# The feed-forward's first product by seven block products in place of eight (decoder layer, one core)

## The chip, the cores and the metric

The kernel runs on one core of a Trainium2 chip. The metric is the device time of one execution in microseconds. The engines are TensorE (PE, with its weight loads PEld), VectorE (DVE), ScalarE (ACT), GpSimd (POOL) and SyncE (SP), which issues most transfers. Each works through its own list of instructions in order and waits at semaphores for the others.

## What is computed

One decoder layer on 8 batches of 256 tokens, width 1024, all in float32: self-attention with sign weights, cross-attention through a low rank, and a low-rank feed-forward, each on a normalised input and added to its stream. The change touches the feed-forward alone:

```python
x = x + _L0_ffn_ref(_layernorm(x, axis=-1), U1, V1, U2, V2, b1, b2)

P = jnp.einsum('bsh,hr->bsr', x, U1)          # 1024 -> 256
H = jnp.einsum('bsr,rf->bsf', P, V1) + b1     # 256 -> 2 x 2752
gate, up = (H[..., :INTER], H[..., INTER:])
act = jax.nn.silu(gate) * up
Z = jnp.einsum('bsi,ir->bsr', act, U2)        # 2752 -> 256
out = jnp.einsum('bsr,rh->bsh', Z, V2) + b2   # 256 -> 1024
```

The product with V1 is the "first product" here: its inner size, 256, is two blocks of 128 (r = 0, 1), and gate and up (i = 0, 1) are two blocks of its rows for each of 21 full groups f of 128 hidden units and one half group of 64.

## The kernel before

**Order.** The program is written under a manual schedule: every engine runs its instructions in the order in which the Python code emits them. Self-attention of all batches comes first, then cross-attention in steps of four heads, then the feed-forward. `step` runs one such step; lists of `Part`s (`cross_plan`) are worked off inside it, so that work of a later stage stands between.

**Feed-forward before.** Tokens go in four blocks of 512 (`fbs`, W = 512). `ffn_x` loads a block's rows of x2 from DRAM. `head_parts` makes its input: `first` normalises the rows on VectorE (`normed_half`, L157), sends them to a DRAM buffer (L1063) and reads them back in quarters (L168); `turn` transposes them in 32x32 squares on VectorE (L1088, 128x512 each); `factor` multiplies by u1 into `ps_p` (L1103) and copies the result to `pT` (even blocks) or `late` (odd blocks).

**One hidden group.** `hidden(fb, k)` takes two PSUM tiles `ps_h` (gate and up) of 512 columns, each the sum of two products, r = 0 and 1 (L1134). ScalarE takes the sigmoid of the gate (L1146), VectorE two three-operand steps on the PSUM tiles (L1147, L1149) that give `ac`. `down` multiplies `ac` by u2 into `ps_z0` and `ps_z1`, which gather over all groups (L1178); the half group is treated by `down_half` (L1158). The main loop keeps `hidden` two groups ahead of `down` (`lag = 2`).

**Tails.** After a block's last group its two `ps_z` are copied to SBUF (L1191); `tail` multiplies by v2 (L1198), adds the token row, to which GpSimd has added b2 (L1480), on VectorE (L1206), and sends it out (L1207). The tails of a block stand between the first groups of the next.

**PSUM.** Eight banks in four pools: `pss` with four buffers (the scores, later `ps_h`), `psA` with two (token products, tails), `psB` and `pso` with one each (`ps_z`).

**Where names recur.** A tile is taken from a pool under a tag; taking a tag again waits until every reader of the tile that held it is done. The tags `qw0` to `qw7` are 128x1024 buffers of 512 KB, in which the token rows stand.

Of the kernel before, what the change touches and what calls it, by code (L numbers as in the profile page):

```python
# [18 lines left out]
P = 128  # L19
# [16 lines left out]
def decoder_layer(  # L36
# [118 lines left out]
    def normed_half(x_, mv, rs, h, tag="xn"):  # L155
        xn = wk_.tile([P, 512], F32, tag=tag, name="xn", bufs=2)
        nc.vector.tensor_scalar(  # L157
            xn, x_[:, h * 512 : (h + 1) * 512], mv, rs, ALU.subtract, ALU.mult
        )
        return xn  # L160
# [862 lines left out]
    def ffn_load_u2():  # L1023
        for k in range(4):
            u2_load(k, xin.tile([P, E], F32, tag="xin", name="u2_sb"))

    def ffn_load_end():
        for k in range(4, (NF + 3) // 4):
            u2_load(k, wk_.tile([P, E], F32, tag=("oh0a", "oh0b")[k - 4], name="u2_sb"))
# [13 lines left out]
    def ffn_x(fb):  # L1043
        while idle:
            idle.pop(0)()
        fb.x = []
        for j in range(BT):
            xs = wt.tile([P, E], F32, tag=f"qw{4 * ((fb.i + 1) % 2) + j}", name="x2t")
            nc.sync.dma_start(xs, x2[fb.i * BT + j])
            fb.x.append(xs)  # L1050

    def head_parts(fb):


        def send(j):
            b = fb.i * 2 + j // TB
            need(fb.half[j // TB])
            for h in range(2):
                xn = normed_half(
                    fb.x[j], mv3[b][:, j % TB, 0:1], rs3[b][:, j % TB : j % TB + 1], h,  # L1060
                    "z" if j % 2 else "xn",
                )
                nc.sync.dma_start(n3[fb.i * BT + j][:, h * 512 : (h + 1) * 512], xn)  # L1063

        def first(m):
            for j in range(2 * m, 2 * m + 2):
                send(j)
            if fb.i == 0 and m == 1:
# [6 lines left out]
            fb.xp = getattr(fb, "xp", {})  # L1075
# [4 lines left out]
        def turn(m):  # L1080
            if m == 0:
                fb.xT = [
                    wk_.tile([P, 4, W], F32, tag="qT", name="xT0", bufs=2),
                    wk_.tile([P, 4, W], F32, tag="xl", name="xT1"),
                ]
            for j in range(2 * m, 2 * m + 2):
                for h in range(2):
                    nc.vector.transpose(  # L1088
                        fb.xT[h][:, :, j * P : (j + 1) * P].rearrange("p c (a q) -> p c a q", q=32),
                        fb.xp[m][j % 2].rearrange("p a (c e) -> p c a e", e=32)[  # L1090
                            :, 4 * h : 4 * h + 4
                        ],
                    )

        def factor(r):
            if r == 0:
                if fb.i % 2 == 0:
                    fb.pT = [wk_.tile([P, W], F32, tag="v", name="pT", bufs=2) for _ in range(RC)]
                else:
                    fb.pT = [fw.late[:, k, :] for k in range(RC)]  # L1100
            ps = psA.tile([P, W], F32, tag="psA", name="ps_p")
            for e in range(EC):
# [3 lines left out]
                    fb.xT[e // 4][:, e % 4, :],  # L1106
# [3 lines left out]
            (dve if r else act)(fb.pT[r], ps)  # L1110

        order = (0, 2, 1, 3) if fb.i == 0 else (0, 1, 2, 3)
        ln = [
            Part(0.0, lambda: first(0)),
            Part(0.0, lambda: turn(0)),
            Part(0.0, lambda: first(1)),
            Part(0.0, lambda: turn(1)),
        ]
        return [ln[k] for k in order] + [Part(7.0, lambda r=r: factor(r)) for r in range(RC)]

    order = list(range(FULL))
    order[FULL - 3 : FULL - 3] = range(FULL, NF)

    def hidden(fb, k):
        f = order[k]
        n = P if f < FULL else LAST
        halves = COPIES if f == FULL else 1
        w_ = W // halves
        hs = []
        for i in range(2):  # L1130
            ps = pss.tile([P, w_], F32, tag="pss", name="ps_h")
            for r in range(RC):
                for h in range(halves):
                    nc.tensor.matmul(  # L1134
                        ps[h * n : h * n + n],
                        v1_of(r, i, f, n),
                        fb.pT[r][:, h * w_ : (h + 1) * w_],
# [4 lines left out]
        m = n * halves  # L1142
        bg = fw.b1[:m, f : f + 1]
        bu = fw.b1[:m, NF + f : NF + f + 1]
        sg = wk_.tile([P, w_], F32, tag="p", name="sg", bufs=4)
        nc.scalar.activation(sg[:m], hs[0][:m], AF.Sigmoid, bias=bg)  # L1146
        nc.vector.scalar_tensor_tensor(sg[:m], hs[0][:m], bg, sg[:m], ALU.add, ALU.mult)  # L1147
        ac = wk_.tile([P, w_], F32, tag="pT", name="ac", bufs=4)
        nc.vector.scalar_tensor_tensor(ac[:m], hs[1][:m], bu, sg[:m], ALU.add, ALU.mult)  # L1149
        return ac, n  # L1150

    def down_half(fb, cross):

        ac, n = fb.half_ac
        w_ = W // COPIES
        for h in range(COPIES):
            r = (h + cross) % RC
            nc.tensor.matmul(  # L1158
                fb.zs[r][:, h * w_ : (h + 1) * w_],
                fw.u2[FULL // 4][h * n : h * n + n, FULL % 4, r * P : (r + 1) * P],  # L1160
                ac[h * n : h * n + n],
                start=False,
                stop=bool(cross),
            )

    def down(fb, k, ac, n):
        if k == 0:
            fb.zs = [
                pso.tile([P, W], F32, tag="pso", name="ps_z0"),
                psB.tile([P, W], F32, tag="psB", name="ps_z1"),  # L1170
            ]
        f = order[k]
        if f == FULL and COPIES == 2:
            fb.half_ac = ac, n
            down_half(fb, 0)
            return
        for r in range(RC):
            nc.tensor.matmul(  # L1178
                fb.zs[r],
                fw.u2[f // 4][:n, f % 4, r * P : (r + 1) * P],  # L1180
                ac[:n],
                start=(k == 0),
                stop=(k == NF - 1 and COPIES < 2),
            )
        if k == NF - 1:
            if COPIES == 2:

                down_half(fb, 1)
            fb.zT = fw.late[:, RC : 2 * RC, :]
            for r, copy in enumerate((dve, act)):  # L1190
                copy(fb.zT[:, r, :], fb.zs[r])  # L1191

    def tail(fb, j, pieces=((0, 512), (512, 512))):
        for c0, n in pieces:
            cols = slice(c0, c0 + n)
            ps = psA.tile([P, n], F32, tag="psA", name="ps_o")
            for r in range(RC):
                nc.tensor.matmul(  # L1198
                    ps,
                    fb.zT[:, r, j * P : (j + 1) * P],  # L1200
# [4 lines left out]
            xs = fb.x[j][:, cols]  # L1205
            nc.vector.tensor_add(xs, ps, xs)  # L1206
            nc.sync.dma_start(of[fb.i * BT + j][:, cols], xs)  # L1207
# [89 lines left out]
    o7, rest, hp0 = [], [], []  # L1297

    def cross_plan(b):
        late = list(rest)  # L1300
        if b + 1 == B:
            return [late + hp0[1:3], hp0[3:4], hp0[4:5], hp0[5:6]]
# [8 lines left out]
        else:  # L1311
            plan = [late + c, k + ln[1:], q + (o[b + 1] if b < 3 else [])]
        rest[:] = u[2:]
        if b + 2 == B:
            hp0[:] = head_parts(fbs[0])
        return plan + [t + u[:2] + (lnx(b + 2)[:1] if b + 2 < B else hp0[:1])]
# [37 lines left out]
    def cross_loads(b, c):  # L1354
        if c == 1 and b + 2 < B:
            cross_c(xts[b + 2])
        if c == 0:
# [5 lines left out]
            if b == 5:  # L1363
                ffn_load_u2()
        if b == B - 2 and c == 2:
            ffn_x(fbs[0])
            ffn_load_v2()
        if b == B - 1 and c == 3:
            ffn_load_b(1)

    with tc.manual_schedule(
# [77 lines left out]
        pairs = [(fb, f) for fb in fbs for f in range(NF)]  # L1449
        acs = {}  # L1450

        def hidden_next(n):
            acs[n] = hidden(*pairs[n])

# [3 lines left out]
        fw.late = None  # L1458
        hidden_next(0)
        prev.weighted(pTs)  # L1460
        hidden_next(1)
        prev.early()
        prev.late()
        ffn_load_end()
        fw.late = wt.tile([P, 2 * RC, W], F32, tag="vw", name="late")
        settle()
        settle()
        lag = 2
        for n in range(2, len(pairs) + lag):
            fb, f = pairs[n] if n < len(pairs) else (None, n)  # L1470
            if fb is not None:
                hidden_next(n)
                if fb.i == 0 and f == 3:
                    x_leave(xts[B - 1])
                elif idle:
                    idle.pop(0)()
                if 10 <= f < 10 + BT:

                    xs = fb.x[f - 10]
                    nc.gpsimd.tensor_add(xs, xs, fw.b2)  # L1480
                if fb.i + 1 < NB:
                    if f == 6:
                        ffn_x(fbs[fb.i + 1])
                    if f == 8:
                        hp = head_parts(fbs[fb.i + 1])
                        queue.extend(hp)
                        queue[0].ahead()
                    for _ in range({9: 1, 11: 2, 13: 1, 14: 1, 15: 1}.get(f, 0)):
                        run_part()
            m = n - lag  # L1490
# [40 lines left out]
```

## Time and profile before

| | us |
|---|---|
| median of three runs (1511.9 to 1512.79) | 1512.69 |
| the profiled execution's own time | 1512.69 |
| its span, from the first to the last instruction | 1510.6 |
| feed-forward in the span (first `ps_h` product to the end) | 957.5 to 1510.6 |
| TensorE busy in the span | 1472.3 |
| VectorE, ScalarE, GpSimd busy | 980.9, 786.3, 398.2 |
| mean granted TensorE clock | 0.997 |

In a row of the groups or the timeline, `out<-in` are the program's tile names; after the shapes come how many, the busy time, the mean duration in ns, and the idle time of the engine before them with what ended it. A row of the timeline begins with its start and its duration in us and merges neighbours ("x2"). A product of 128x128 weights with 512 float32 columns stands in the trace as two matmul records.

### The profile page before, as it was taken

To read this page: it belongs to the slowest core of one execution; us is meant where nothing else is said; L and a number is where in the kernel's file an instruction comes from. 1 tells how busy PE (TensorE), PEld (TensorE's weight loads), DVE (VectorE), ACT (ScalarE), POOL (GpSimd) and SP (SyncE) were. 2 spreads that over 40 slices of the span, in tenths; PEclk is the share of its full clock that TensorE was granted. 3 is DMA by queue.
4 is the path that set the end of the run, shared out by engine and by line. 5 is a ranking of instruction groups with operands and counts; after the bars stand their busy time and mean duration, and the time that the engine had idled before them with its cause. 6 is when DMAs were issued, how large, how long until landed. Compare 5 with 4: busy or idle time off the path is not lost.

```text
span 1510.6 us, 25435 instructions
## 1 busy us (share of the span) xinstructions
PE 1472.3 (97%) x9118; PEld 981.2 (65%) x9118; DVE 980.9 (65%) x1911; ACT 786.3 (52%) x2429; POOL 398.2 (26%) x472
## 2 busy tenths in 40 slices
PE   6899999999999999899999999999999999999999
PEld 6777888888888886677777776444444444444444
DVE  6888898999999888867787776354335233523332
ACT  4778898989898987746566666310111110111110
POOL 2544454535453545123231211141002000200000
PEclk9999999999999999999999999999999999999999
DMA  8520020101010134334486755132014002300001
GB/s 214 122 57 30 15 71 29 57 30 57 30 62 24 57 106 154 101 98 116 142 259 207 198 169 164 63 97 57 0 64 152 7 15 97 112 0 28 28 0 56
DMA packets 102958, 126.33 MB, mean 84 GB/s; under 512 B 44539, under 2 KB 75441, under 8 KB 102705
## 3 DMA queue, kind: packets, MB, share of 16 engines
q1 hardware_dynamic: 98224, 107.94, 24.8%
q0 software_dynamic: 4608, 16.78, 2.8%
q8 instruction: 72, 1.18, 0.3%
q14 instruction: 54, 0.43, 0.1%
HBM read 82.21 MB, written 41.94 MB: 82 GB/s over the span
## 4 chain that ended last, share of the span: by engine, by line
PE 55%; ACT 2%; DVE 2%; DMA 1%; issue 0%; SPq 0%; ACTq 0%; DVEq 0%
PE ps_h L1134 20%; PE ps_z L1178 10%; PE ps_pt L579 4%; PE ps_o L1198 4%; PE ps_p L1103 4%; PE s L676 3%; PE po L699 3%; PE ps_o L716 2%; PE ps_q L925 2%; ACT p L762 2%; PE ps_qk L941 2%; PE ps_k L855 1%; PE ps_o L547 1%; DMA n<-xn 0%; PE ps_z L1158 0%
## 5 line engine op out<-in xcount | busy, mean ns | idle before, releaser
L762 ACT ACTIVATE p<-s,nm 128x256 f32<-128x256 f32 x768 | 359.0, 519 | 4.4 <-DVE nm L743 4.4
L1146 ACT ACTIVATE sg<-ps_h,b_col 128x512 f32<-128x512 f32 (+1 forms) x88 | 59.6, 678 | 427.6 <-PE ps_h L1134 427.5
L583 ACT COPY pT<-ps_pt 128x512 f32<-128x512 f32 x384 | 197.4, 599 | 147.0 <-PE ps_pt L579 147.0
L743 DVE TENSOR_REDUCE nm<-s 128x2 f32<-128x512 f32 x384 | 237.2, 676 | 4.6 <-PE s L676 3.4
L1147 DVE SCALAR_TENSOR_TENSOR sg<-ps_h,b_col,sg 128x512 f32<-128x512 f32 (+1 forms) x88 | 64.8, 736 | 241.9 <-ACT sg L1146 241.9
L579 PE MATMUL ps_pt<-ident,p 128*128 128x128 f32 x1536 | 197.4, 280 | 7.3 <-ACT pT L583 2.8
L579 PEld LDWEIGHTS ps_pt<-ident,p 128*128 128x128 f32 x1536 | 165.9, 142 | 47.8 <-issue 24.3
L762 ACT ACTIVATION_READ_ACCUMULATOR p<-s,nm 128x1 f32 x768 | 192.7, 251 | 0.0
L1178 PE MATMUL ps_z<-ac,u_sb 128*128 128x512 f32 x336 | 158.0, 593 | 0.0
L454 PE MATMUL ps_q<-xh,qT_w 128*128 128x256 f32 x496 | 121.7, 287 | 0.0
L454 PE MATMUL ps_q<-xl,qT_w 128*128 128x256 f32 x496 | 118.8, 281 | 0.0
L1178 PEld LDWEIGHTS ps_z<-ac,u_sb 128*128 128x128 f32 x336 | 63.5, 190 | 80.0 <-issue 80.0
L1480 POOL TENSOR_TENSOR x2t<-x2t,b_sb 128x1024 f32<-128x1024 f32 x16 | 38.8, 2436 | 272.3 <-DVE xn L157 272.3
L547 PE MATMUL ps_o<-oT_w,oh 128*128 128x512 f32 x256 | 105.5, 412 | 0.0
L731 POOL TENSOR_TENSOR x1t<-x1t,y 128x256 f32<-128x256 f32 x64 | 46.2, 742 | 221.2 <-DVE y L724 221.2
L407 POOL TENSOR_SCALAR tmp<-y 128x512 f32<-128x512 f32 x78 | 58.5, 751 | 166.3 <-DVE y L556 91.2
L547 PE MATMUL ps_o<-oT_w,ol 128*128 128x512 f32 x256 | 101.0, 395 | 0.0
L454 PEld LDWEIGHTS ps_q<-xh,qT_w 128*128 128x128 f32 x496 | 93.3, 188 | 1.7
L454 PEld LDWEIGHTS ps_q<-xl,qT_w 128*128 128x128 f32 x496 | 93.4, 188 | 0.0
L623 DVE TENSOR_SCALAR p<-p,sm 128x256 f32<-128x256 f32 x256 | 86.8, 396 | 8.4 <-PE ps_q L454 0.5
L1134 PE MATMUL ps_h<-pT,w_ffn 128*128 128x512 f32 (+1 forms) x184 | 88.7, 577 | 0.0
L1134 PE MATMUL ps_h<-late,w_ffn 128*128 128x512 f32 (+1 forms) x184 | 88.7, 577 | 0.0
(156 smaller groups left out, 2648.5 us busy)
## 6 DMA issues: line engine op xcount, KB each, us to landing
xs<-in_x_dram SPq DMA_DIRECT2D x32, 512.0 KB
n<-xn SPq DMA_DIRECT2D x64, 256.0 KB
xp<-n SPq DMA_DIRECT2D x128, 128.0 KB
x<-xs POOLq DMA_DIRECT2D x16, 512.0 KB, 3.1
x1t<-x SPq DMA_DIRECT2D x16, 512.0 KB
c<-in_ctx_dram SPq DMA_DIRECT2D x64, 128.0 KB
x<-x1t POOLq DMA_DIRECT2D x16, 512.0 KB, 5.3
x2t<-x SPq DMA_DIRECT2D x16, 512.0 KB
```

Source lines behind the costliest of these rows:

```text
L454: nc.tensor.matmul(ps[:, i, :], w(i, e), x_[:, e, :], start=(e == 0 and x_ is st.xh), stop=(e == EC - 1 and x_ is st.xl),)
L547: nc.tensor.matmul(ps, o_[c // 4][:, c % 4, t * P : (t + 1) * P], oT_w[:, c, h * 512 : (h + 1) * 512], start=(c == 0 and o_ is st.oh), sto ...
L579: nc.tensor.transpose(ps[:, k, t * P : (t + 1) * P], p[:, t, k * P : (k + 1) * P], ident)
L583: nc.scalar.copy(pT, ps)
L623: nc.vector.tensor_scalar_mul(p, p, self.sm[:, t, j : j + 1])
L743: nc.vector.tensor_reduce(nm[:, j, :], s[j], AX.X, ALU.max, negate=True)
L762: nc.scalar.activation(cur.p[j][:, t, :], s[j][:, t, :], AF.Exp, bias=nm[:, j, t : t + 1], accum_out=cur.sm[:, t, j : j + 1],)
L1103: nc.tensor.matmul(ps, fw.u1[:, e, r * P : (r + 1) * P], fb.xT[e // 4][:, e % 4, :], start=(e == 0), stop=(e == EC - 1),)
L1134: nc.tensor.matmul(ps[h * n : h * n + n], v1_of(r, i, f, n), fb.pT[r][:, h * w_ : (h + 1) * w_], start=(r == 0), stop=(r == RC - 1),)
L1147: nc.vector.scalar_tensor_tensor(sg[:m], hs[0][:m], bg, sg[:m], ALU.add, ALU.mult)
L1178: nc.tensor.matmul(fb.zs[r], fw.u2[f // 4][:n, f % 4, r * P : (r + 1) * P], ac[:n], start=(k == 0), stop=(k == NF - 1 and COPIES < 2),)
L1198: nc.tensor.matmul(ps, fb.zT[:, r, j * P : (j + 1) * P], fw.v2[:, r, cols], start=(r == 0), stop=(r == RC - 1),)
```

## The change

The feed-forward goes over two blocks of 1024 tokens (`dbs`), each two halves of 512. With A the 2x2 blocks of V1 (gate and up by r) and B the 2x2 blocks of P (r by half), the four results are formed from seven products (Winograd's form of Strassen's scheme) by `unit`. Sums of weight blocks are formed on GpSimd one unit ahead (`weight_sums`), sums of token blocks once for each 1024 tokens on VectorE (`sums`). Three of the products gather in one PSUM tile `c21`, which ScalarE reads out between them. In the listing `act` is a ScalarE copy, `stt` a VectorE three-operand step, `mul` a GpSimd multiplication:

```python
def weight_sums(db, f):
    ...
    g.tensor_add(s_[:, 0, :], a[1][0], a[1][1])
    g.tensor_sub(s_[:, 1, :], s_[:, 0, :], a[0][0])
    g.tensor_sub(s_[:, 2, :], a[0][0], a[1][0])
    g.tensor_sub(s_[:, 3, :], a[0][1], s_[:, 1, :])

def sums(db):
    ...
    sub(db.t1, b12, b11)
    sub(db.t2, b22, db.t1)
    sub(db.t3, b22, b12)
    sub(db.t4, b21, db.t2)

def unit(db, k, following):
    ...
    extra = max(0, len(zq) - 4)
    product(c21, v1_of(0, 0, f, P), b11, True, False)      # c21a
    act(a1, c21)
    product(c11, v1_of(1, 0, f, P), b21, True, True)       # c11
    trailing()
    stt(g1, c11, bg, a1, ALU.add, ALU.add)
    fill(1 + (extra > 0))
    product(c21, s_[:, 1, :], db.t2, False, False)         # c21b
    nc.scalar.activation(sg1, g1, AF.Sigmoid)
    act(q, c21)
    product(c12, s_[:, 0, :], db.t1, True, False)          # c12a
    fill(1 + (extra > 1))
    product(c21, s_[:, 2, :], db.t3, False, False)         # c21c
    act(q7, c21)
    mul(g1, g1, sg1)
    stt(ac2, c12, bu, q7, ALU.add, ALU.add)
    if following is not None:
        weight_sums(*following)
    fill()
    product(c21, v1_of(1, 1, f, P), db.t4, False, True)    # c21d
    stt(g1, c21, bu, g1, ALU.add, ALU.mult)
    fill()
    product(c12, s_[:, 3, :], b22, False, True)            # c12b
    stt(g2, c12, bg, q, ALU.add, ALU.add)

    def rest():
        nc.scalar.activation(sg2, g2, AF.Sigmoid)
        mul(g2, g2, sg2)
        mul(ac2, ac2, g2)

    trail.append(rest)
    for t, ac in ((0, g1), (1, ac2)):
        for r in range(RC):
            zq.append(lambda t=t, r=r, ac=ac: down(db, k, r, t, ac))
```

(The names behind the products are added here for reference.) `fill` issues the next waiting product with u2 from `zq`; `trailing` emits the `rest` of the unit before. The half group (`half_unit`) stays a direct product, now over 2 x 512 tokens. The four `ps_z` of 1024 tokens take `psA`, `psB` and `pso`; token products and tails move to `pss`. Transposes become 128x128 pieces; the normalisation of the first two blocks of 512 moves to GpSimd and to the last two cross-attention steps' lists, that of the others stays on VectorE, with the tag `xn` (two buffers) alone. The rows of x2 are loaded a second time for the tails:

```diff
+    def tail_x(db, j, tag):
+        xs = wt.tile([P, E], F32, tag=tag, name="x2t")
+        nc.sync.dma_start(xs, x2[db.i * 2 * BT + j])
+        nc.gpsimd.tensor_add(xs, xs, fw.b2)
+        db.x = getattr(db, "x", {})
+        db.x[j] = xs
```

The main loop after the change:

```diff
-        lag = 2
-        for n in range(2, len(pairs) + lag):
...
+            return {
+                2: lambda: x_leave(xts[B - 1]),
+                4: lambda: ffn_x(fbs[2], 0),
+                5: lambda: f2[0].main(),
+                6: lambda: ffn_x(fbs[2], 1),
+                7: lambda: (turns(t2_, 0), f2[1].main()),
+                9: lambda: turns(t2_, 1),
+                10: lambda: ffn_x(fbs[3], 0),
+                11: lambda: (p2[0].main(), f3[0].main()),
+                12: lambda: (p2[1].main(), ffn_x(fbs[3], 1)),
+                14: lambda: (turns(t3_, 0), f3[1].main()),
+                16: lambda: turns(t3_, 1),
+            }.get(k, lambda: None)
+
+        for k in range(FULL):
+            if k == FULL - 3:
+                half_unit(d0)
+            unit(d0, k, (d0, units[k + 1]) if k + 1 < FULL else (d1, units[0]))
+            if idle:
+                idle.pop(0)()
+            between(k)()
+        trailing()
+        for j in range(3):
+            tail_x(d0, j, f"qw{j}")
+        p3[0].main()
+        p3[1].main()
+        for k in range(FULL):
+            if k == FULL - 3:
+                half_unit(d1)
+            unit(d1, k, (d1, units[k + 1]) if k + 1 < FULL else None)
+            if 1 <= k < 1 + 2 * BT:
+                tail(d0, k - 1)
+                if k + 2 < 2 * BT:
+                    tail_x(d0, k + 2, f"qw{(k + 2) % 3}")
+            if 12 <= k < 16:
+                tail_x(d1, k - 12, ("qw0", "qw1", "qw2", "qw4")[k - 12])
+        for j in range(4, 8):
+            tail_x(d1, j, ("qw3", "qw5", "qw6", "qw7")[j - 4])
+        trailing()
+        fill(len(zq))
+        for j in range(2 * BT - 1):
+            tail(d1, j)
+        tail(d1, 2 * BT - 1, ((0, 512), (512, 256), (768, 128), (896, 128)))
```

Here `f2`, `t2_`, `p2` are the normalisation, transposes and token products of the third block of 512, `f3`, `t3_`, `p3` those of the fourth. Of the second block of 1024, the first half's b11 and b21 stand in `qw3`, b12 and b22 in `qw5`, the sums t1 and t3 in `qw6`, t2 and t4 in `qw7`.

## The prediction

> **What bounds the kernel now.** I read the page's head and the stretches first, then the chain that ended last, then the timeline of one hidden unit, then the groups on GpSimd, and last the DMA issues.
>
> ```profile
> span 1510.6 us, 25435 instructions
> PE 1472.3 (97%) x9118; PEld 981.2 (65%) x9118; DVE 980.9 (65%) x1911; ACT 786.3 (52%) x2429; POOL 398.2 (26%) x472
> ```
> ```profile
> 1050.00:1100.00 50.00, 50.00 (x133) 21.93 (x132) 14.36 (x20) 6.56 (x10) 0.00 (x0) 1.00 0.00 0
> 1450.00:1511.00 61.00, 56.85 (x155) 25.44 (x153) 18.02 (x27) 5.87 (x9) 0.00 (x0) 0.99 0.09 35
> ```
>
> The columns of a stretch are its length, then the busy time of PE, PEld, DVE, ACT and POOL. From 950 us on this is the feed-forward: TensorE never rests, VectorE works 30% of the time, ScalarE 13%, GpSimd nearly nothing. A matmul taken out there is time saved, as long as nothing else becomes late.
>
> ```profile
> 1210.43 1.02 PE L1134 MATMUL ps_h<-late,w_ffn 128*128 128x512 f32 x2
> 1210.63 0.69 ACT L1146 ACTIVATE sg<-ps_h,b_col 128x512 f32<-128x512 f32 x1 [4.01 <-PE ps_h L1134]
> 1211.29 1.02 PE L1134 MATMUL ps_h<-late,v1b 128*128 128x512 f32 x2
> 1211.35 0.75 DVE L1147 SCALAR_TENSOR_TENSOR sg<-ps_h,b_col,sg 128x512 f32<-128x512 f32 x1 [3.62 <-ACT sg L1146]
> 1212.14 1.88 PE L1178 MATMUL ps_z<-ac,u_sb 128*128 128x512 f32 x4
> ```
>
> A product of 128x128 by 512 columns is two records, and products start 0.86 us apart (1210.43, 1211.29). A reader starts 0.20 us after the issue of the product ends (the product before 1210.43 gates the 1210.63). Release of TensorE by VectorE costs 0.06: copy of ps_z ends 1493.24, next matmul 1493.30.
>
> **What goes.** 21 full units x 2 blocks of 1024 tokens x 1 product = 42 x 0.86 = 36.0 us. The half unit took 1205.01 to 1206.89, 1.88 x 4 = 7.5, and its second product 0.63 x 8 = 5.0; now they are 8 and 4 pairs of 0.86, 10.3 together: 2.2 less. The 0.8 us in which the last product waits for the copy of ps_z goes too, as other work now stands between. Removed: **39.0 us**.
>
> **One unit, step by step.** TensorE's order in it, starts from 0: c21a 0, c11 0.86, z 1.72, c21b 2.57, c12a 3.43, z 4.29, c21c 5.15, z 6.01, c21d 6.86, z 7.72, c12b 8.58, end 9.44. The z are the last unit's products with u2. Durations: ScalarE copy from PSUM 0.59 (ps_z, L1191), sigmoid 0.69, VectorE's three-operand step 0.75, GpSimd as below.
>
> ```profile
> L408 POOL TENSOR_TENSOR z<-z,tmp 128x512 f32<-128x512 f32 x32 | 42.5, 1329 | 2.7
> L1480 POOL TENSOR_TENSOR x2t<-x2t,b_sb 128x1024 f32<-128x1024 f32 x16 | 38.8, 2436 | 272.3 <-DVE xn L157 272.3
> ```
>
> So a multiplication of 128x512 on GpSimd is 1.32, an addition of 128x1024 2.36 (its median), a weight sum of 128x128 some 0.45 (0.742 at 256 columns, 1.329 at 512).
> - ScalarE: copy a1 1.06 to 1.65; the trailing sigmoid of the unit before to 2.34 (its input is ready at 1.1 + 0.2); sg1 after g1 (VectorE 1.92 to 2.67), 2.7 to 3.39; copy q 3.63 to 4.22; copy q7 6.21 to 6.80.
> - c21b may start when a1 is read: 0.9 us to spare. c21c needs q: 0.9 to spare. c21d needs q7: 6.86 against 6.86, nothing to spare.
> - GpSimd: the two trailing multiplications 2.4 to 5.0, g1 to 6.4, four weight sums to 8.2. The third z needs the trailing result: 5.0 against 6.01.
>
> A unit thus fits in 9.44. Only the tight q7 costs: bounds 0 and 0.3 x 42 = 12 us, I take 0.05 x 42 = **2**.
>
> **VectorE between the units of the first block of 1024.** Normalisation and transposes for the second are put behind units 5, 7, 9, 11, 14 and 16, ahead of the next unit's g1, sg1 and q, which queue in this order. A burst of X starts at 0.95 of the next unit (behind g2), so q ends at 0.95 + X + 0.75 + 0.03 + 0.69 + 0.59 = 3.0 + X, and c21c, due at 5.15, stalls X - 2.1.
>
> ```profile
> 1149.07 3.94 DVE L157 TENSOR_SCALAR xn<-x2t,mv,rs 128x512 f32<-128x512 f32 x4
> 1150.20 2.53 POOL L1480 TENSOR_TENSOR x2t<-x2t,b_sb 128x1024 f32<-128x1024 f32 x1 [121.67 <-DVE xn L157]
> ```
>
> Four normalised halves took 3.94 while GpSimd was at work (median of one 0.54, so 2.2 alone). Now GpSimd works in every unit and the halves have two buffers, not four; I take 3.9, bounds 2.2 and 5.5 (twice the wait seen). The transposes become 16 of 128x128 for 4 of 128x512 (0.62 each in a row): between a quarter of it, 2.5, and a 128x128 copy each, 16 x 0.28 = 4.5; I take 16 x 0.22 = 3.5. Statistics add 0.7 to the first.
> - behind 5: 4.6, stalls 2.5; behind 7 and 14: 7.4, stalls 5.3 each; behind 9 and 16: 3.5, stalls 1.4 each; behind 11 a token product of 6.9 us on TensorE covers it. Together **16**, bounds 5 and 28. This cover was there before: a unit's results were wanted two units later.
>
> [...]
>
> **The first unit** has no z to fill with, and its g1 stands behind four VectorE sums and y (0.8 + 2.6 + 0.7 = 4.1 after the last token product), the table load of 1.28 (once in the trace) and sg1: q ends at 7.3, c21c was due at 4.6 (1.15 of ps_o and four products); then c21d waits 0.9. **3.6**, bounds 2 and 6.
>
> **The tails of the first block of 1024.** Behind units 1 to 5 of the second block stand a tail of token tile k-1 (four products, 3.43), then a load of x2 into the buffer that this tail just emptied, and GpSimd's addition of b2 to it. On GpSimd this addition stands ahead of the trailing multiplications, for which the third z of the next unit waits.
>
> ```profile
> 1129.52 0.69 DVE L1206 TENSOR_TENSOR x2t<-ps_o,x2t 128x512 f32<-128x512 f32 x1 [0.95 <-PE ps_o L1198]
> ```
> ```profile
> 1130.66 2.13 SPq L1049 DMA_DIRECT2D x2t<-x  x4
> ```
> ```profile
> 4.26 1.29 DVE L140 BATCH_NORM_STATS2 st<-xs 128x6 f32<-128x512 f32 x2 [4.26 <-DMA xs<-in_x_dram]
> ```
>
> The last addition ends at 1130.21; the last of four loads into those buffers is issued by about 1132.4, so an output of 256 KB lands within 2.2. A load of 512 KB: issued at 0.73 at the kernel's start, first read at 4.26: 3.5; bounds 2.2 (the output) and 5.3 (GpSimd's own 512 KB writes, the page's median). From the unit's end: tail 3.43, its last addition 3.63 to 4.32, output landed 6.6, load landed 10.15, b2 added 12.55, two multiplications 15.2. The third z is due at 3.43 + 6.01 = 9.44: a stall of 5.8 us, five times = **29**; with the bounds 22 and 38.
>
> [...]
>
> **The end.** Four such additions stand ahead of the last unit's two trailing multiplications. The second of their loads goes into the buffer of b12 and b22, which c12b frees at 9.44: landed 13.1, three additions to 20.2, multiplications to 22.8. The third z was due at 9.44 + 1.72 = 11.16. **11.7**, bounds 10 and 15; nothing is behind it but the tails, which wait for it.
>
> **Elsewhere.** The token products of the second half block move into the last cross step; they use the score buffers and wait for the exponentials (0.8 each, twice), and the second block's first q is late by 0.4: **2**, bounds 0 and 5. The small transposes there stand beside TensorE's 7.5 to 14 us per step.
>
> **Sum.** -39.0 + 2 + 16 + 3.6 + 29 + 11.7 + 2 = +25.3. The profiled execution took 1512.7 (span 1510.6), which is also the median of the three runs: 1538. With all lower bounds -39 + 0 + 5 + 2 + 22 + 10 + 0 = 0, with all upper ones -39 + 12 + 28 + 6 + 38 + 15 + 5 = +65.
>
> **Rivals.**
> 1. Faster: GpSimd's additions of b2 do not hold the multiplications back, in the tails and at the end. The five stalls are gone and the end costs only the chain of g2, 0.75 + 0.69 + 2.64 less two z of 0.86, some 2.4: -39 + 2 + 16 + 3.6 + 2.4 + 2 = -13, 1500. It decides from where the addition starts 9.44 - 2.64 - 2.36 = 4.44 us behind the unit's end. Against it: the tail's own last addition, before output and load, ends at 4.32. For it: only the place of the load would have to differ from what I read, as at units 12 to 15, whose buffers have long been free. Chance 0.10.
> 2. All waits hidden, VectorE's bursts too: 1512.7 - 39 + 6 = 1480. The lag of one unit for z speaks against it. Chance 0.05.
> 3. Heavier: halves and GpSimd's steps stretch each other, loads take 5 us, q7 costs 0.3 each time: +45 to +65, 1565. For it: 1149.07 above. Chance 0.14.
> 4. The sums cancel: chance 0.04 within 3 us (0.2%, about what a measurement of this kernel can tell from no change).
>
> **How the numbers follow.** The forecast, 1518 to 1556, has 0.67. Slower by over 0.2%: 0.67 + 0.14 = 0.81; same 0.04; faster 0.15. The range leaves out rivals 1 and 2 and the worst third of rival 3: 1508 to 1562.
>
> **What would show it.** Right: in the second block of 1024 five gaps of about 6 us on TensorE ahead of a z, with GpSimd in the addition of b2 or waiting for its load; a gap of some 12 us before the last two z; gaps ahead of c21c behind units 7 and 14 of about 5 us; otherwise units of 9.4 us. Wrong: five such units as short as 12.9 us (with a tail), or stalls in every unit ahead of c21d.

## The result, and the profile after

The changed kernel took 1557.29 us (median of four, 1555.47 to 1558.59), the kernel before 1512.74 (four, 1511.9 to 1514.49) beside it: a ratio of 1.0292, 95% interval 1.0274 to 1.031. The forecast was 1538 with a range of 1508 to 1562: slower, as forecast, and 19 us more than forecast. The profiled execution took 1558.59, its span 1556.8; its mean granted clock is 0.971 (0.997 before).

First the page of the changed kernel, for the two lines that the prediction began with:

```profile
span 1556.8 us, 25823 instructions
PE 1463.0 (94%) x8986; PEld 969.0 (62%) x8986; DVE 973.4 (63%) x1991; ACT 851.4 (55%) x2557; POOL 659.3 (42%) x782
```

The span grew by 46.2. TensorE's idle time grew from 38.3 to 93.8, by 55.5; its busy time fell by 9.3 only, although 39.0 of products were taken out. So two things happened: TensorE waits, which the forecast had priced, and some products take longer, which it had not. The stretches show both (length, then PE, PEld, DVE, ACT, POOL busy, the granted clock, the DMA share, GB/s):

```profile
1050.00:1100.00 50.00, 44.09 (x95) 18.66 (x94) 22.23 (x55) 11.44 (x20) 22.82 (x30) 0.92 0.28 89
1100.00:1150.00 50.00, 50.00 (x117) 21.63 (x116) 13.27 (x19) 12.84 (x22) 21.71 (x28) 1.00 0.21 64
1250.00:1300.00 50.00, 39.62 (x81) 16.78 (x80) 11.10 (x16) 7.57 (x13) 20.28 (x23) 0.86 0.12 42
```

The middle row is a stretch of undisturbed units: TensorE full, clock 1.00. The first holds two of VectorE's bursts, the last two of the tails: there TensorE is idle for 6 and 10 us, and its granted clock, the mean over the stretch, is 0.92 and 0.86 of full speed. Now the timeline of the changed kernel around the first of the five tails:

```profile
1260.27 0.69 DVE L1323 TENSOR_TENSOR x2t<-ps_o,x2t 128x512 f32<-128x512 f32 x1 [1.02 <-PE ps_o L1315]
1263.02 0.33 SPq L1304 DMA_DIRECT2D x2t<-x  x1
1266.53 2.35 POOL L1305 TENSOR_TENSOR x2t<-x2t,b_sb 128x1024 f32<-128x1024 f32 x1 [11.56 <-DMA x2t<-x]
1268.82 1.27 POOL L1236 TENSOR_TENSOR g<-g,sg 128x512 f32<-128x512 f32 x1
1270.17 1.26 POOL L1237 TENSOR_TENSOR ac<-ac,g 128x512 f32<-128x512 f32 x1
1271.48 2.07 PE L1290 MATMUL ps_z<-ac,u_sb 128*128 128x512 f32 x2 [5.24 <-POOL ac L1237]
1273.35 1.91 PE L1196 MATMUL c<-t,v1b 128*128 128x512 f32 x2
1275.06 1.67 PE L1290 MATMUL ps_z<-ac,u_sb 128*128 128x512 f32 x2
1276.57 1.02 PE L1196 MATMUL c<-pT,s_v 128*128 128x512 f32 x2
```

Read it from the top: the tail's last addition, the load of x2 (issued once the output has left the buffer), GpSimd's addition of b2 (GpSimd had been idle for 11.56 us, the last part of it for that load), the two multiplications behind it, and the third z, which waited 5.24 us. This is the forecast's chain, step for step. What it lacks is in the last four rows. The four products start 1.87, 1.71 and 1.51 us apart, not 0.86: TensorE runs at half its rate behind the gap, and gets its rate back about 5 us later. That is 2.5 us more for each such gap.

Next a burst of VectorE in the first block of 1024, again the timeline of the changed kernel:

```profile
1063.09 3.19 DVE L1111 STREAM_TRANSPOSE xT<-xp 128x128 f32<-128x128 f32 x16
1066.21 1.62 DVE L157 TENSOR_SCALAR xn<-x2n,mv,rs 128x512 f32<-128x512 f32 x2
1069.54 1.18 DVE L157 TENSOR_SCALAR xn<-x2n,mv,rs 128x512 f32<-128x512 f32 x2 [1.71 <-DMA n<-xn]
1072.01 0.57 ACT L1213 COPY q<-c 128x512 f32<-128x512 f32 x1
1072.72 2.04 PE L1196 MATMUL c<-t,s_v 128*128 128x512 f32 x2 [5.19 <-ACT q L1213]
```

Sixteen transposes and four halves come to 7.5 us (7.4 in the forecast). c21c waits 5.19 us for q (5.3) and then takes 2.04 instead of 1.02. The halves are slow mostly by their two buffers: 1.71 us of waiting for a send. The one half that begins beside a GpSimd multiplication (1065.82 to 1067.09) took 1.16 us, the other three 0.54 to 0.55.

A third gap was not in the forecast in this size. It lies in the last cross-attention step:

```profile
930.71 8.24 POOL L157 TENSOR_SCALAR xn<-x2n,mv,rs 128x512 f32<-128x512 f32 x4
948.65 0.89 DVE L1111 STREAM_TRANSPOSE xT<-xp 128x128 f32<-128x128 f32 x4 [7.19 <-DMA xp<-n]
950.99 0.89 DVE L1111 STREAM_TRANSPOSE xT<-xp 128x128 f32<-128x128 f32 x4 [1.45 <-DMA xp<-n]
951.89 0.64 DVE L709 COPY ol<-po 128x512 f32<-128x512 f32 x1
952.67 2.05 PE L716 MATMUL ps_o<-w_up,ol 128*128 128x128 f32 x8 [6.72 <-DVE ol L709]
```

Normalised on GpSimd, a half takes 2.06 us (8.24 for four). The rows go out and come back late, VectorE waits 7.19 and then 1.45 us for them ahead of two groups of transposes, and the copy ol, which TensorE needs, stands behind these.

### The profile page after: what moved, and what is told of

It reads as the page before. It is cut to its first block, busy times and chain, and to the rows that moved or that the text cites. A ratio compares the mean times of both kernels' runs of the same rounds, so it can differ in the third digit from the quotient of the medians.

```text
span 1556.8 us, 25823 instructions
## 1 busy us (share of the span) xinstructions
PE 1463.0 (94%) x8986; PEld 969.0 (62%) x8986; DVE 973.4 (63%) x1991; ACT 851.4 (55%) x2557; POOL 659.3 (42%) x782
## 5 line engine op out<-in xcount | busy, mean ns | idle before, releaser
L579 PEld LDWEIGHTS ps_pt<-ident,p 128*128 128x128 f32 x1536 | 167.2, 143 | 46.2 <-issue 24.6
L1202 ACT COPY a<-c 128x512 f32<-128x512 f32 x42 | 24.6, 586 | 210.9 <-PE c L1196 210.9
L1196 PE MATMUL c<-t,s_v 128*128 128x512 f32 x252 | 124.3, 602 | 14.8 <-ACT q L1213 14.2
L1222 DVE SCALAR_TENSOR_TENSOR ac<-c,b_col,q 128x512 f32<-128x512 f32 x42 | 31.5, 751 | 169.7 <-ACT q L1219 169.7
L1290 PE MATMUL ps_z<-ac,u_sb 128*128 128x512 f32 x168 | 97.2, 667 | 37.6 <-POOL ac L1237 37.6
L407 POOL TENSOR_SCALAR tmp<-y 128x512 f32<-128x512 f32 x78 | 59.3, 760 | 166.9 <-DVE y L556 91.3
L1236 POOL TENSOR_TENSOR g<-g,sg 128x512 f32<-128x512 f32 x42 | 53.4, 1271 | 169.2 <-ACT sg L1235 169.2
L1196 PEld LDWEIGHTS c<-t,s_v 128*128 128x128 f32 x252 | 47.7, 192 | 77.2 <-issue 73.1
L1290 PEld LDWEIGHTS ps_z<-ac,u_sb 128*128 128x128 f32 x168 | 35.7, 217 | 85.8 <-POOL ac L1237 43.6
```

The source lines that it names most:

```text
L407: nc.gpsimd.tensor_scalar(tmp, y, 0.0, -1e6, ALU.min, ALU.max)
L579: nc.tensor.transpose(ps[:, k, t * P : (t + 1) * P], p[:, t, k * P : (k + 1) * P], ident)
L1196: nc.tensor.matmul(ps, w, x_, start=start, stop=stop, skip_group_check=True)
L1236: mul(g2, g2, sg2)
L1290: nc.tensor.matmul(db.zs[t][r], fw.u2[f // 4][:, f % 4, r * P : (r + 1) * P], ac, start=(k == 0), stop=last,)
```

## The experiments

Every kernel was timed against the kernel before on the same chip, which took 1513.01 beside numbers 1, 2, 3 and 5, 1512.81 beside 4, 6, 7 and 8, and 1515.01 beside 9 and 10. The theory is the forecast's, with a clock term added: TensorE waits at known places, and each longer wait is followed by some 5 us at half rate. Differences to the changed kernel are taken to its 1557.29; gaps and unit lengths are those of the one profiled execution of each kernel. The rivals stand in each expectation.

**1. The multiplications ahead of the additions of b2** (tails and end):

```diff
             if 1 <= k < 1 + 2 * BT:
+                trailing()
                 tail(d0, k - 1)
...
+        trailing()
         for j in range(4, 8):
             tail_x(d1, j, ("qw3", "qw5", "qw6", "qw7")[j - 4])
-        trailing()
```

> GpSimd's two trailing multiplications are put ahead of its additions of b2, behind units 1 to 5 and at the end; nothing else changes. My theory (the multiplications wait behind an addition that waits for its load): the five gaps of 5.1 to 5.5 us go, with the slowed products behind each (2.5 us), 39 us; the last gap falls from 11.3 to the g2 chain of 2.6 us, some 10 us with the slowed products. 1508 us. Rival (the additions and loads are late anyway and the next multiplication of g1 then waits in their place): at most 10 us less, 1547 to 1557.

Measured: 1508.79, ratio to before 0.9971 (0.996 to 0.9982). The five gaps are gone and the end's gap is 2.53 instead of 11.28. GpSimd's timeline at the same tail:

```profile
1257.04 1.27 POOL L1236 TENSOR_TENSOR g<-g,sg 128x512 f32<-128x512 f32 x1 [3.41 <-ACT sg L1235]
1258.39 1.27 POOL L1237 TENSOR_TENSOR ac<-ac,g 128x512 f32<-128x512 f32 x1
1265.11 2.35 POOL L1305 TENSOR_TENSOR x2t<-x2t,b_sb 128x1024 f32<-128x1024 f32 x1 [5.45 <-DMA x2t<-x]
```

The addition waits for its load as before, but nobody waits for it. The gain of 48.5 us is 26.3 (the five gaps) + 8.8 (the end's) + 13.4 (slow products: 12.0 behind the five gaps, 1.4 at the end, from the profiles) = 48.5.

**2. The load earlier instead, into a fourth buffer:**

```diff
-                tail(d0, k - 1)
                 if k + 2 < 2 * BT:
-                    tail_x(d0, k + 2, f"qw{(k + 2) % 3}")
+                    tail_x(d0, k + 2, ("qw0", "qw1", "qw2", "qw4")[(k + 2) % 4])
+                tail(d0, k - 1)
```

> The order on GpSimd stays, but the load and the addition of b2 for tile k+2 are put ahead of the tail of tile k-1 and go to a fourth buffer, so that the addition has no output and no load to wait for. The end is untouched. My theory (the round trip of output and load is the price, the addition itself fits): the five gaps go with what follows them, 39 us less, 1518 us. Rival (the addition of 2.35 us itself is too much for GpSimd in a unit): some 12 us of gaps stay, 1530 us or more.

Measured: 1518.57, ratio 1.0037 (1.0022 to 1.0052): 38.7 us less, against 26.3 + 12.0 for the five gaps with their slow products; the end's gap stays at 11.18. So the addition holds the multiplications back only through its load, as the forecast had it.

**3. Gaps filled with products that nobody reads**, ahead of the third z of units 2 to 6 of the second block:

```diff
+        if db.i == 1 and 2 <= k < 7:
+            spare = bank_("spare")
+            for _ in range(6):
+                product(spare, v1_of(0, 0, f, P), b11, True, True)
         fill()
```

> Six products that nobody reads are put ahead of the third z of units 2 to 6 of the second block of 1024: 5.2 us of TensorE work in the place of each gap of 5.2 us. Theory (a gap costs twice: its own length, and a halved TensorE clock for some 3.4 us of products behind it): the gaps are filled at no cost and the products behind them keep their 0.86 us, 5 x 2.5 = 12 us less, 1545 us, granted clock 0.98 or more. Rival (the products behind a gap are slow because GpSimd works on SBUF then): they stay slow, 1557 us or more.

Measured: 1545.94, ratio 1.0221 (1.0205 to 1.0238). The third z comes no earlier and 30 products are added, yet the kernel is 11.4 us faster. This separates the two costs of a gap: the wait is untouched, and the half rate behind it (12.0 us by the units' lengths) is gone.

**4. The same with three products for six:**

```diff
-            for _ in range(6):
+            for _ in range(3):
```

> Three products that nobody reads stand ahead of the third z of units 2 to 6 of the second block of 1024: they fill 3 x 0.86 = 2.6 us of each gap of 5.2 and leave 2.6 us. If what slows TensorE behind a gap is the length of the gap, and 2.6 us is too short for it, the five gaps' slow products go as with six such products, and the time is 1546. If any gap over 1 or 2 us has this effect, the slow products stay and the time is that of the changed kernel, 1557. In between: 1550 means that a gap of 2.6 us costs a part.

Measured: 1551.78, ratio 1.0251 (1.0232 to 1.0271), in between. Gaps of 2.49 to 2.98 us remain; one of the five is without slow products, four have them. Two of them in the timeline of this kernel:

```profile
1289.79 1.13 PE L1294 MATMUL ps_z<-ac,u_sb 128*128 128x512 f32 x2 [2.49 <-POOL ac L1241]
1290.76 1.02 PE L1196 MATMUL c<-t,v1b 128*128 128x512 f32 x2
...
1308.06 1.43 PE L1294 MATMUL ps_z<-ac,u_sb 128*128 128x512 f32 x2 [2.55 <-POOL ac L1241]
1309.28 1.91 PE L1196 MATMUL c<-t,v1b 128*128 128x512 f32 x2
```

2.49 and 2.55 us, and the one costs nothing more while the other does. Both theories on the length alone have fallen; see the last section.

**5. VectorE's bursts cut up**: sends, loads and transposes spread over units 2 to 19, one to three pieces behind a unit.

```diff
-                5: lambda: f2[0].main(),
-                7: lambda: (turns(t2_, 0), f2[1].main()),
...
+                4: lambda: g2.send(0),
+                5: lambda: (g2.send(1), g2.load(0), ffn_x(g2, 1)),
+                6: lambda: g2.send(2),
+                7: lambda: t2_[0, 0].main(),
+                8: lambda: (t2_[0, 1].main(), ffn_x(g3, 0)),
```

> The normalisation, loads and transposes of the second block of 1024 are cut into pieces of one token tile or eight transposes and spread over units 2 to 19, so that hardly any burst on VectorE exceeds 2.1 us. My theory (a burst of X stalls c21c by X - 2.1): the gaps of 2.35, 5.19, 0.72, 5.19, 0.72 us go but for about 1 us behind two longer pieces, and the slowed products behind the three long ones: 14 + 7 - 2 = 19 us less, 1538 us. Rival (the work is only moved, the same VectorE time delays g1 in more units): 1550 to 1557.

Measured: 1543.6 (1540.37 to 1544.13), ratio 1.0204 (1.0187 to 1.0221). The profiled execution did what was expected (1540.37, its span 18.2 less than the changed kernel's; gaps of 1.29 and 1.89 in place of 14.2 us in five). The median fell by 13.7 only: of both kernels' profiled executions, the changed kernel's is the slowest of its four and this one the fastest of its four. The other three took 1543.36 to 1544.13 and have no trace. Their granted clocks are on record, 0.977 to 0.979 against 0.978 in the profiled one, and so do not speak for more slow products in them; what makes them 3 to 4 us longer stays open.

**6. Normalisation of the first two blocks of 512 on VectorE again:**

```diff
-                    nc.gpsimd if fb.i < 2 else nc.vector,
+                    nc.vector,
```

> The normalisation of the first two blocks of 512 is on VectorE again instead of GpSimd. If GpSimd's four times 2.06 us in the last cross-attention step is what VectorE, and behind it TensorE, waited for, the gap of 6.72 us ahead of the first feed-forward products goes, and about 2.5 us of slow products behind it: 1548. If VectorE is short of time itself in these steps, as the move to GpSimd supposes, the gap stays or others come up in the last two cross-attention steps: 1557 or more.

Measured: 1551.41 (1548.32 to 1554.41), ratio 1.0248 (1.022 to 1.0276): 5.9 us less, some 3 short of what was expected. The gap falls from 6.72 to 1.88 (it is 5.34 to 7.80 in the six profiled kernels that keep these halves on GpSimd) and does not go. VectorE's timeline of this kernel says why:

```profile
940.96 0.89 DVE L1111 STREAM_TRANSPOSE xT<-xp 128x128 f32<-128x128 f32 x4 [6.06 <-DMA xp<-n]
944.12 0.64 DVE L709 COPY ol<-po 128x512 f32<-128x512 f32 x1
```

The four halves now take 1.88 us, but VectorE still waits 6.06 us for the rows' return, with ol behind it.

**7. Numbers 1, 5 and 6 together:**

> Multiplications ahead of the additions of b2, pieces spread over the units, and normalisation on VectorE, all at once. If each removes its own gaps and the slow products behind them, the effects add: 1557.3 - 48.5 - 13.7 - 9 = 1486; without the third 1495. If the lower clock comes from how closely the products are packed, and not from the gaps, TensorE slows somewhere else and no more than half of it adds: 1500 or more.

Measured: 1488.79 (1487.5 to 1490.62), ratio 0.9836 (0.9816 to 0.9855). That is 68.5 us less than the changed kernel, where the three gains measured alone come to 48.5 + 13.7 + 5.9 = 68.1: the effects add. The clock does not give way elsewhere: it is 0.992.

**8. As 7, with two of a unit's z between c21c and c21d:**

```diff
-        fill()
+        fill(2)
         product(c21, v1_of(1, 1, f, P), db.t4, False, True)
         stt(g1, c21, bu, g1, ALU.add, ALU.mult)
-        fill()
```

> As the one before, and two of each unit's z stand between c21c and c21d, none ahead of c12b, so that the copy q7 has 0.86 us more. If c21d's lateness of about 0.09 us in each of 42 units is the copy q7, 3.8 us go: 1482. If it is something else (weight loads, records), nothing changes: 1486. If c12b then comes too early for the reader of c12's first part (ac2 on VectorE), it is slower: 1490.

Measured: 1489.43, ratio 0.9843 (0.982 to 0.9865), no difference in the median. In the trace the unit did shrink, from 9.53 to 9.44 us (starts of the copy a1), but two gaps of the profiled execution had grown: the one in the last cross-attention step from 2.46 to 4.58, the one behind unit 8 from 1.29 to 2.52. So two more kernels, without the first of these.

**9 and 10. As 7 (number 9) and as 8 (number 10), with two more edits in both**: the transposes that wait stand behind ol, with the weighted sums ahead of the token product; the last unit's multiplications are on VectorE.

```diff
-                p0[:1] + [t1_[0, 0], t1_[1, 0]],
-                p0[1:] + [t1_[0, 1], t1_[1, 1]],
+                p0[:1] + [t1_[0, 0], t1_[0, 1]],
+                p0[1:],
...
         prev.prev.late()
-        heads[1][2][0].main()
+        heads[1][1][1, 0].main()
+        heads[1][1][1, 1].main()
         prev.weighted(pTs)
         prev.early()
+        heads[1][2][0].main()
...
+            m = nc.vector.tensor_mul if following is None else mul
```

> All three edits together, z as in the change, and two more: the last four transposes of the second block of 512, which wait for a transfer, stand behind the copy ol on VectorE instead of ahead of it, with the first token product behind the weighted sums; and the last unit's two multiplications are on VectorE. If the transposes' wait was handed on through VectorE's order, the gap of 2.46 us in the last cross-attention step goes, and the gap of 2.53 us before the last z falls by 2 x (1.3 - 0.7) = 1.2: 1485. If the transfer itself is what is late, the gap only moves to the token product behind it: 1488.

> The same, with two of each unit's z between c21c and c21d and none ahead of c12b. If c21d's lateness is the copy q7, and only the wider gap in the last cross-attention step hid this gain before, it is 4 us faster than the one with the z of the change: 1481. If the gain is given back elsewhere in the unit, both are equal.

Measured: 1484.48 (1481.87 to 1487.68; ratio 0.9804, 0.9788 to 0.982) and 1480.81 (1479.08 to 1484.97; ratio 0.9777, 0.9763 to 0.979). The cross-attention gap is 0.51 and 0.52, the end's 1.30 and 0.97, the units 9.53 and 9.44, which over 42 units is some 3.6 us. The medians differ by 3.7, but the two kernels' times overlap, and the profiled execution of number 10 is the longer one: its gap behind unit 8 is 2.52 us for 1.39, and one more gap is followed by slow products. So it is the length of the unit that shows this gain, not the times. The last kernel beats both kernels of this case. Its page and one of its stretches:

```profile
span 1483.2 us, 25825 instructions
PE 1440.6 (97%) x8986; PEld 965.8 (65%) x8986; DVE 981.0 (66%) x2009; ACT 852.4 (57%) x2557; POOL 624.7 (42%) x764
```
```profile
1250.00:1300.00 50.00, 50.00 (x118) 22.23 (x117) 15.24 (x23) 11.71 (x20) 29.84 (x29) 1.00 0.24 84
```

The same 8986 matmul records as in the changed kernel take 22.4 us less of TensorE's busy time, and the stretch of the tails is full at clock 1.00.

## Why the prediction was right, and where its size was wrong

Term by term, in us, predicted and as the profiled execution of the changed kernel shows it:

| term | predicted | measured |
|---|---|---|
| products removed | -39.0 | (taken as it stands) |
| q7 too tight, 42 units | 2 | 3.8 (units of 9.53, not 9.44) |
| VectorE's bursts | 16 | 14.2 (2.35, 5.19, 0.72, 5.19, 0.72) |
| first unit | 3.6 | 1.3 (0.62, 0.68) |
| five tails | 29 | 26.3 (5.13 to 5.46 each) |
| end | 11.7 | 11.3 |
| elsewhere | 2 | 6.7 (last cross-attention step) |
| sum | +25.3 | +24.6 |
| slow products behind the gaps | none | 21.6 (the rest of +46.2) |

- **The places were right.** Waits of the forecast's kind stood where it put them, behind the engines that it named. Numbers 1 and 2 show that the additions of b2, and through them their loads, made the tails' gaps.
- **The failing step is a missing term.** The sum priced each stall as idle time and let every product behind it cost 0.86. Behind the gaps the products cost up to twice that. Measured by the lengths of the units: 12.0 us in the five tail units (20.4 to 20.8 us each; 12.96 without gap, in number 1) beyond their gaps, 7.4 behind the three larger bursts, 1.4 at the end: 20.8 of the 21.6. The granted clock gives the same without the sum: from 900 us on the changed kernel's TensorE is busy for 42.1 us at half clock, of which half, 21.0, is lost, and the kernel before for none. Number 3 shows the 12.0 by itself as 11.4. The mean clocks of the two pages, 0.971 and 0.997, say a little more than that: between 100 and 650 us, far ahead of the feed-forward, 7.7 us are lost against 2.6, and the kernels of the experiments, which share that part with the changed kernel, vary there from 2.5 to 7.8.
- **How long the half rate lasts.** The feed-forward of the kernel before did not show it: from 900 us on its longest gap on TensorE is 1.53 us, and no product there runs at half clock. The changed kernel's trace has half rate behind each gap of 5.1 to 5.5 us, at a cost of 2.2 to 3.0 us for each, since the products are slow for 4.1 to 5.7 us (number 3 expected some 3.4): the half clock, 0.50, lasts 6.83 us each time and begins inside the gap.
- **Inside the range, partly by luck.** The range reached 1562 because the stalls were given wide upper bounds, and the bursts, the tails and the end stayed well below these (14.2 for 28, 26.3 for 38, 11.3 for 15). What took the room above 1538 is a term that the sum did not have. Two small terms left their own bounds: elsewhere (6.7, bound 5) and the first unit (1.3, bound 2). The bounds of the bursts, 5 and 28, do not come out of the pieces given for them, which make 6.8 and 24.7.
- **The first unit, 3.6 against 1.3.** The sum put the table load of 1.28 us (the trace before has two, one of them in the feed-forward) behind y and g1. In the trace it runs beside them (table load 985.09 to 986.37, y and g1 985.16 to 986.50).
- **Elsewhere, 2 against 6.7.** Normalisation on GpSimd was not priced: 2.06 us a half. Number 6 took 4.8 us of this gap away by undoing it, and 9 most of the rest (0.51 is left, and 0.49 at the next product) by the order on VectorE: the rows' return was not late for TensorE, only for a copy that stood behind it.
- **q7.** The forecast had found nothing to spare there and took 0.05; it is 0.09, and the units' lengths in numbers 8 and 10 show that two z ahead of c21d remove it.
- **The rivals.** Rival 1 was the case that the additions do not hold the multiplications back, 1500. Number 1 makes it true and gives 1508.79; the 9 us between are mostly the slow products behind the bursts (5.6 in its profile, by the units' lengths) and the cross-attention gap (7.1 there, where 2 was priced). Rival 3, 1565, came nearest in time for another reason than its own: the five tails' loads took 3.2 to 3.3 us from issue to landing, not 5, and the bursts cost 14.2 us, not the 28 of the upper bound. Rival 2's 1480 is what the kernel takes once six edits have taken most waits away (1480.81, number 10).

## What to carry to other kernels

When a change takes TensorE's work away and adds waits, price each wait twice: the idle time, and the slower products behind it, here 2.2 to 3.0 us for every gap of some 5 us; gaps of 1.89 to 2.55 us had slow products behind them in some places and none in others (next section). Before the saving is written off, look at what stands between a late producer and its reader in the order of each engine: here six edits of order and place, with no less work, turned 45 us slower into 34 us faster. A gain that does not show in the median can still be seen in the length of the repeated unit.

## What was not expected of the hardware

- TensorE's rate behind a gap is not a matter of the gap's length alone. Gaps of 5.1 to 5.5 us between units were followed by slow products every time. The same gap of 2.35 us behind unit 5 was so in one profile and not in five others; here the changed kernel and number 3, timelines of TensorE:

```profile
1046.63 1.10 PE L1196 MATMUL c<-t,s_v 128*128 128x512 f32 x2 [2.35 <-ACT q L1213]
1047.57 1.80 PE L1290 MATMUL ps_z<-ac,u_sb 128*128 128x512 f32 x2
```
```profile
1045.96 1.10 PE L1196 MATMUL c<-t,s_v 128*128 128x512 f32 x2 [2.35 <-ACT q L1213]
1046.90 1.02 PE L1294 MATMUL ps_z<-ac,u_sb 128*128 128x512 f32 x2
```

  In number 9 a gap of 1.89 us was followed by products of 1.64, 1.91 and 1.37 us, in number 10 by slow ones too, in numbers 5, 7 and 8 the same gap by none. Gaps of 0.7 us were never followed by one. The granted clock in the traces shows where they differ. In all twelve it is either full (1.00) or half (0.50), and within a trace all its changes lie on one raster of 3.413 us; a field of it is the time between two neighbouring points. Here are two neighbouring fields of the raster for each of the two gaps above, first the changed kernel, then number 3 (columns as in the stretches above):

```profile
1044.26:1047.67 3.41, 1.06 (x4) 0.59 (x4) 1.03 (x2) 1.10 (x2) 1.58 (x2) 1.00 0.74 242
1047.67:1051.08 3.41, 3.41 (x6) 1.30 (x5) 0.75 (x1) 0.58 (x1) 1.37 (x4) 0.50 0.84 191
```
```profile
1044.34:1047.75 3.41, 1.79 (x4) 0.69 (x5) 0.32 (x2) 1.69 (x3) 2.25 (x4) 1.00 0.97 304
1047.75:1051.16 3.41, 3.41 (x9) 1.61 (x9) 2.01 (x3) 0.00 (x0) 0.70 (x2) 1.00 0.93 210
```

  In the changed kernel the gap lies wholly in one field, which leaves TensorE 1.06 us of work there, and the next field has half the clock. In number 3 a boundary of the raster cuts the gap, 1.79 us of work are left, and the clock stays full. This holds without exception from 900 us on in the twelve traces: behind each of the 52 fields at full clock in which TensorE was busy for at most 0.450 of the time the clock fell to half, and it fell behind none with 0.451 or more. It came back behind every field busy for 0.83 or more, and behind none of up to 0.76. The ends of products are modelled in the trace, so the share that divides the two is 0.45 or near it. The two gaps of number 4, 2.49 and 2.55 us, left 1.89 and 0.87 us of work in their emptier fields; the 1.89 us of numbers 7 and 9 left 1.54 and 1.52. An estimate from these numbers: 0.55 of a field is 1.88 us, so in traces like these a single gap under that would cost no clock, one over twice that (3.75 us) would cost it wherever it lies, and one between by where it lies. No run here moved a gap against the raster on purpose, and none shows where the raster comes from.
- A normalisation of 128x512 with two operands per partition took 2.06 us on GpSimd, where a step with constants took 0.76 (L407, the mean of 78) and VectorE's own about 0.5: four in 1.88.
